# Weighing the next block's query terms inside the attention loop, and one pair sum moved between the halves of a reciprocal

## The chip, the core and the metric

The kernel runs on one core of a Trainium2 chip. Five engines matter here: TensorE (PE in the profile; its weight loads are PEld), VectorE (DVE), ScalarE (ACT), GpSimd (POOL) and SyncE (SP, which here only issues DMAs). Each engine works through its own instructions in order; semaphores tie them together. The metric is device time in microseconds of one launch. Before the change it is 10633.31 us, the median of three runs (10629.44 to 10641.02).

## The reference

The input is `x` of shape (4, 128, 64, 64). Layer 0 normalises it by groups and adds a convolution with a selective scan. Layer 1 reads the result as 4 images of 4096 tokens with 128 channels and adds two terms. The first of them, an additive attention, is what this change touches:

```python
def _L1_attn_ref(x, Wt, Wx, bh, Wa, ba):
    q = jnp.einsum('bld,ud->blu', x, Wt)
    k = jnp.einsum('bld,ud->blu', x, Wx)
    beta = jnp.tanh(q[:, :, None, :] + k[:, None, :, :] + bh)
    alpha = jnp.einsum('bsju,u->bsj', beta, Wa[:, 0]) + ba[0]
    alpha = jnp.tanh(alpha)
    alpha = jax.nn.softmax(alpha, axis=-1)
    c_r = jnp.einsum('bsj,bjd->bsd', alpha, x)
    return c_r
```

There are 32 hidden units u, and for every image 4096 x 4096 pairs (s, j), so the sum over u of `Wa[u] * tanh(q + k)` dominates. The second term is a recurrence over the tokens, in the function `_chunked`.

## The kernel before

Three functions follow one another: `_layer0`, `_rational` (the attention) and `_chunked` (the recurrence). The order of the instructions in each is written out by hand: what the Python code issues first comes first in its engine's queue.

**How the tanh is avoided.** The 32 hidden units are split into six groups, two of 6 units and four of 5. Within a group, the weighted sum of the tanh is a quotient of two sums of exponentials, one term for each choice of signs: 64 terms for 6 units, 32 for 5. Each term is a product of a factor of the query and a factor of the key. So for keys `F = exp(...)` and queries `E = exp(...)`, the denominator of a group is one matmul of F with E (tile `pd`), and the numerator is the same matmul with `cE`, which is E with each row multiplied by that term's weight `c_n` (tile `pn`). The function `weigh` makes `cE` from `E` with two VectorE instructions.

**The tiling.** A block is 512 queries (`QB`) of one image; there are 8 blocks for each of 4 images, 32 in all. Within a block the code goes through the 4096 keys in 32 tiles of 128 (`jt`). For each `jt` there are three units: "A" (the two groups of 6), "B1" and "B2" (two groups of 5 each). A unit's tile is 128 keys x 2 groups x 512 queries.

**The loop over the units.** For unit i, PE makes the denominators two units ahead and the numerators one unit behind. ACT inverts the denominator as exp(-ln d): line 1524 is the Ln, which also empties `pd`; line 1527 is the Exp, one unit later. DVE multiplies with the two numerators (`times`, line 1414, two instructions for a unit). POOL adds the units B1 and B2 to A (line 1533), which leaves two sums side by side, and DVE adds these to one another (`whole`, line 1518) and so finishes one row `A[:, jt, :]`. The tile of a unit A comes from the pool `ra` (4 buffers), that of a unit B from the pool `rb` (5 buffers).

`whole` for tile `jt - 1` is issued right after the second unit of tile `jt` has been multiplied, so that the loop itself finishes the tiles up to JT - 2 = 30.

**Work hung into the loop.** The dictionary `between` names small steps and the place (jt, position in jt) after which each is issued; `later` fills it. Here stand the matmuls, the maximum and the Exp of the next block's queries (`E_next`, from place (23, 2) and (25, 2) on), the layer norm of the next image, the last products of the block before with the values (`weighted`), and that block's closing division and its addition on POOL (line 1462).

**The end of a block.** After the loop, `weigh(E_next)` makes `cE` for the next block (line 1379). Then ACT takes the softmax's Tanh and Exp over the 32 finished rows in four parts (`PARTS`: rows 0 to 4, 12, 20 and 32; lines 1583 and 1584). Meanwhile `ahead` starts the next block: it makes the denominators of its first key tile and inverts them on DVE with `direct`, which takes a unit's two halves one after the other, each a reciprocal (line 1424) and a product with the numerator (line 1425). The sum `whole(31)` is issued once, after the first of these halves. Between the calls of `ahead`, PE does the products with the values of the parts that are already done (`weighted`, line 1557). `ahead(3)` ends with the denominators of the first two units of the next loop. In three of the 31 block ends the image changes, and then `all_keys` computes the next image's keys before `ahead`.

**Memory.** The pools of `_rational` are opened in a fixed order and lie in SBUF one after the other in that order; the pool `one` (1 buffer) holds `cE`, `two` (2 buffers) holds `xn` and `E`, `fp` holds F.

Of the kernel before, what the change touches and what calls it, by code (L numbers as in the profile page):

```python
# [8 lines left out]
F32 = mybir.dt.float32  # L9
# [6 lines left out]
P = 128  # L16
# [10 lines left out]
JT = L // P  # L27
# [36 lines left out]
QB = 512  # L64
# [1177 lines left out]
def _rational(ctx, tc, k, x1, xn1, x2, top, kept, ba):  # L1242
# [11 lines left out]
    one = ctx.enter_context(tc.tile_pool(name="none", bufs=1))  # L1254
    sb = ctx.enter_context(tc.tile_pool(name="nsb", bufs=2))
    ra = ctx.enter_context(tc.tile_pool(name="nra", bufs=4))
    rb = ctx.enter_context(tc.tile_pool(name="nrb", bufs=5))
    two = ctx.enter_context(tc.tile_pool(name="ntwo", bufs=2))
    fp = ctx.enter_context(tc.tile_pool(name="nf", bufs=1))
    kp = ctx.enter_context(tc.tile_pool(name="nk", bufs=1))  # L1260
    psD = ctx.enter_context(tc.tile_pool(name="npsD", bufs=2, space=PSUM))
    psN = ctx.enter_context(tc.tile_pool(name="npsN", bufs=3, space=PSUM))
# [111 lines left out]
        return exponent(pw, w_q, xn[:, s * QB : (s + 1) * QB], i, E[:, i, :])  # L1374

    def weigh(E):
        cE = one.tile([P, 2, QB], F32, name="cE")
        for i in range(2):
            nc.vector.tensor_scalar(cE[:, i, :], E[:, i, :], c_n[:, i : i + 1], None, ALU.mult)  # L1379
        return cE  # L1380
# [36 lines left out]
        pool, tag = (ra, "ra") if unit == "A" else (rb, "rb")  # L1417
        return pool.tile([P, 2, QB], F32, name=tag, tag=tag)

    def direct(d, ns, unit, then=None):  # L1420

        r = ratio(unit)
        for a in range(2):
            nc.vector.reciprocal(r[:, a, :], d[:, a, :])  # L1424
            nc.vector.scalar_tensor_tensor(r[:, a, :], r[:, a, :], 1.0 / LOWER, ns[a], ALU.mult, ALU.mult)
            if then is not None:
                then()
                then = None
        return r

    def order(jt):
# [50 lines left out]
    cE = weigh(E)  # L1482
# [8 lines left out]
    for b in range(B):  # L1491
        upcoming = None
        for s in range(nq):
# [11 lines left out]
            if more:  # L1505
                E_next = two.tile([P, 2, QB], F32, name="E")
                of = upcoming if turned else xn
                for i in range(2):
                    later(between, 23 + 2 * i, 2, zip(queries(E_next, of, (s + 1) % nq, i), (0, 1, 2)))
            ln_exp()  # L1510
            units = [(jt, pos, unit) for jt in range(start, JT) for pos, unit in enumerate(order(jt))]
            n = len(units)
            D = dict(enumerate(first))
# [6 lines left out]
            for i in range(n + 2):  # L1520
# [7 lines left out]
                if i >= 2:  # L1528
                    at, p, unit = units[i - 2]
                    r = R[at, p]  # L1530
                    times(r, N.pop(i - 2))
                    if p:
                        nc.gpsimd.tensor_tensor(R[at, 0], R[at, 0], R.pop((at, p)), ALU.add)  # L1533
                    if p == 1 and at > start:
                        whole(at - 1)
                forms = []
                if i + 2 < n:
# [12 lines left out]
            assert not between  # L1550

            if more:
                E, cE = E_next, weigh(E_next)
            ct = pw()

            def weighted(jt, ct=ct, xT=xT):
# [1 line left out]

            held = {}

            def ahead(step):
                if not more:
                    if step == 0:
                        whole(JT - 1)
                    return
                if step == 0:
                    held["A"], held["B1"] = lower("A", F, 0, E), lower("B1", F, 0, E)
                    held["A"] = direct(held["A"], upper("A", F, 0, cE), "A", lambda: whole(JT - 1))  # L1570
                elif step == 1:
                    held["B2"] = lower("B2", F, 0, E)
                    held["B1"] = direct(held["B1"], upper("B1", F, 0, cE), "B1")
                    nc.gpsimd.tensor_tensor(held["A"], held["A"], held["B1"], ALU.add)
                elif step == 2:
                    held["first"] = lower("A", F, 1, E)
                    r = direct(held["B2"], upper("B2", F, 0, cE), "B2")
                    nc.gpsimd.tensor_tensor(held["A"], held["A"], r, ALU.add)
                else:
                    held["first"] = held["first"], lower("B2", F, 1, E)  # L1580
# [283 lines left out]
```

## Time and profile before

| | |
|---|---|
| median of three runs | 10633.31 us |
| the profiled execution | 10622.87 us, span 10621.1 us |
| busy, of the span | PE 9213.9, DVE 9043.7, ACT 9094.5, POOL 8609.3 us |
| mean granted clock of TensorE | 0.942 of full speed |
| `_rational` | from about 3606 to about 10357 us of the span |
| one block, loop and end (block 7) | loop 177.67 us (5087.27 to 5264.94), end before it 30.42 us (5056.85 to 5087.27) |
| Ln, line 1524, into `rb` and `ra` | 1230 and 1219 ns each; ACT idle before them 26.9 and 52.6 us in all |
| `times`, line 1414 | 682 to 686 ns |
| `whole`, line 1518 | 759 ns, 993 times |
| POOL's sum, line 1533 | 2519 ns, 1986 times |
| `weigh`, line 1379 | 64 times, 479 to 2590 ns, median 1411 ns |

The profile is of one execution. Busy time is the time in which an engine worked; a duration of an instruction that follows closely on another can include some of its neighbour. "Idle before" is the time in which the engine stood still ahead of an instruction, and the arrow names what it waited for last. PE's clock is throttled by the hardware at times; the profile shows the share that was granted.

### The profile page before, as it was taken

How to read it: one execution, taken by the hardware profiler on the slowest of the kernel's cores; microseconds unless marked ns; L12 is line 12 of the kernel's file. 1: busy time of each engine (PE TensorE's matmuls, PEld its weight loads, DVE VectorE, ACT ScalarE, POOL GpSimd, SP SyncE). 2: the span in 40 equal slices, each digit the busy share in tenths (PEclk: the TensorE clock that was granted, in tenths of full speed). 3: DMA queues.
4: the chain of work that ended last, by engine and by line, in shares of the span. 5: the costliest groups of instructions: out<-in, count | busy, mean ns of one | idle time of the engine just before them, and what ended most of it. 6: DMA issues, size and time to landing. Idle time of an engine off the chain costs nothing.

```text
span 10621.1 us, 110120 instructions
## 1 busy us (share of the span) xinstructions
PE 9213.9 (87%) x35452; PEld 3226.5 (30%) x35452; DVE 9043.7 (85%) x10031; ACT 9094.5 (86%) x10279; POOL 8609.3 (81%) x3686
## 2 busy tenths in 40 slices
PE   7787787787777799999999999999999999999997
PEld 2121221222211233333333333333333333333334
DVE  7999999999999788888888888888888888888882
ACT  4566666766766799999999999999999999999995
POOL 7999899999999777788678778877888777767773
PEclk8898898898888999999999999999999999999998
DMA  6889889888888200000000000000000000000001
GB/s 150 200 191 213 189 193 212 194 197 209 198 199 203 71 4 4 4 4 7 4 4 4 7 4 4 7 4 4 4 7 4 4 3 5 3 3 3 5 2 66
DMA packets 228573, 739.50 MB, mean 70 GB/s; under 512 B 41536, under 2 KB 42368, under 8 KB 226448
## 3 DMA queue, kind: packets, MB, share of 16 engines
q1 hardware_dynamic: 224576, 730.76, 29.2%
q8 instruction: 280, 4.59, 0.2%
q14 instruction: 309, 2.53, 0.1%
q10 hardware_dynamic: 3408, 1.63, 0.1%
HBM read 609.15 MB, written 118.88 MB: 69 GB/s over the span
## 4 chain that ended last, share of the span: by engine, by line
PE 35%; ACT 21%; DVE 5%; issue 5%; POOL 1%; DMA 0%; DVEq 0%; POOLq 0%; ACTq 0%; SPq 0%
PE pd L1393 16%; PE pn L1393 10%; PE ct L1557 6%; ACT rb L1527 6%; ACT rb L1524 6%; ACT ra L1524 2%; ACT A L1583 2%; DVE rb L1414 2%; ACT ra L1527 2%; ACT A L1584 1%; DVE ra L1424 1%; PE vy L1758 1%; POOL ra L1533 0%; DVE cE L1379 0%; ACT E L1300 0%
## 5 line engine op out<-in xcount | busy, mean ns | idle before, releaser
L1533 POOL TENSOR_TENSOR ra<-ra,rb 128x1024 f32<-128x1024 f32 x1986 | 5000.9, 2519 | 813.0 <-ACT rb L1527 446.5
L1393 PE MATMUL pn<-cE,F 32*128 32x512 f32 (+1 forms) x12288 | 4602.5, 643 | 88.3 <-DVE rb L1414 78.0
L1393 PE MATMUL pd<-E,F 32*128 32x512 f32 (+1 forms) x12288 | 4037.8, 650 | 342.9 <-ACT ra L1524 239.8
L1414 DVE TENSOR_TENSOR rb<-rb,pn 128x512 f32<-128x512 f32 x3972 | 2543.4, 682 | 582.4 <-PE pn L1393 576.8
L1527 ACT ACTIVATE rb<-rb 128x1024 f32<-128x1024 f32 x1986 | 2513.6, 1270 | 0.0
L1524 ACT ACTIVATE rb<-pd 128x1024 f32<-128x1024 f32 x1986 | 2443.0, 1230 | 26.9 <-PE pd L1393 24.6
L786 POOL TENSOR_TENSOR dBu<-dtdu,bbcc 128x1024 f32<-128x1024 f32 x1024 | 2391.4, 2365 | 88.8 <-DMA dtdu<-dd 58.2
L1393 PEld LDWEIGHTS pd<-E,F 32*128 32x128 f32 (+1 forms) x12288 | 1209.9, 186 | 2257.2 <-ACT ra L1524 972.1
L1393 PEld LDWEIGHTS pn<-cE,F 32*128 32x128 f32 (+1 forms) x12288 | 1420.9, 186 | 1317.3 <-DVE rb L1414 647.0
L1414 DVE TENSOR_TENSOR ra<-ra,pn 128x512 f32<-128x512 f32 x1986 | 1356.1, 686 | 384.8 <-PE pn L1393 287.4
L826 PE MATMUL py<-h,gather 128*32 128x512 f32 x4096 | 1190.6, 677 | 391.7 <-POOL h L812 372.9
L1527 ACT ACTIVATE ra<-ra 128x1024 f32<-128x1024 f32 x993 | 1258.0, 1267 | 0.0
L1524 ACT ACTIVATE ra<-pd 128x1024 f32<-128x1024 f32 x993 | 1210.4, 1219 | 52.6 <-PE pd L1393 43.7
L781 ACT ACTIVATE pa<-dtdu,a_neg 128x1024 f32<-128x1024 f32 x1024 | 1143.6, 1117 | 34.7 <-DMA dtdu<-dd 11.2
L802 DVE TENSOR_TENSOR_SCAN pa<-pa,carry,dBu 128x1024 f32<-128x1024 f32 x480 | 1125.4, 2345 | 32.3 <-ACT pa L781 22.9
L1557 PE MATMUL ct<-A,xT 128*128 128x512 f32 x2048 | 1046.4, 639 | 10.5 <-ACT A L1584 10.5
L812 POOL TENSOR_TENSOR h<-h,bbcc 128x1024 f32<-128x1024 f32 x381 | 899.3, 2360 | 121.8 <-ACT carry L810 104.9
L810 ACT COPY carry<-pa 128x1 f32<-128x1 f32 x643 | 103.0, 160 | 883.9 <-DVE h L809 883.3
L809 DVE TENSOR_TENSOR h<-pa,bbcc 128x1024 f32<-128x1024 f32 x643 | 787.7, 1225 | 61.7 <-PE py L826 1.7
L1518 DVE TENSOR_TENSOR A<-ra 128x512 f32<-128x512 f32 x993 | 753.9, 759 | 35.9 <-POOL ra L1533 31.6
L802 DVE TENSOR_TENSOR_SCAN h<-pa,carry,dBu 128x1024 f32<-128x1024 f32 x288 | 673.2, 2341 | 21.3 <-PE py L826 10.6
L826 PEld LDWEIGHTS py<-h,gather 128*32 128x32 f32 x4096 | 221.8, 116 | 1255.9 <-issue 529.0
(306 smaller groups left out, 8282.2 us busy)
## 6 DMA issues: line engine op xcount, KB each, us to landing
bbcc<-bcd SPq DMA_DIRECT2D x1024, 256.0 KB, 7.7
dtdu<-ddd SPq DMA_DIRECT2D x1008, 256.0 KB, 7.8
ddd<-dd SPq DMA_DIRECT2D x63, 1024.0 KB, 5.1
src<-src SPq DMA_DIRECT2D x60, 512.0 KB, 9.7
xs<-in_x_dram SPq DMA_DIRECT2D x32, 256.0 KB, 7.3
src<-xs SPq DMA_DIRECT2D x16, 512.0 KB, 6.2
bcd<-bc SPq DMA_DIRECT2D x64, 128.0 KB, 1.9
src<-xsT SPq DMA_DIRECT2D x16, 512.0 KB, 5.4
```

What stands on the lines that cost most here:

```text
L781: nc.scalar.activation(dA, its[m].DT[r][:, 0, :], AF.Exp, scale=a)
L786: nc.gpsimd.tensor_tensor(dBu, its[m].DT[r][:, 1, :], its[m].BC[q][:, 0, :], ALU.mult)
L802: nc.vector.tensor_tensor_scan(to[:, step], dA[:, step], live.pop(("dBu", u))[:, step], 0.0 if m % nch == 0 else its[m - 1].carry[:, col : ...
L809: nc.vector.tensor_tensor(h, dA, cc, ALU.mult)
L812: nc.gpsimd.tensor_tensor(h, h, cc, ALU.mult)
L826: nc.tensor.matmul(it.y[to, c], gather, live["h", v][:, c], start=False, stop=(q == QS - 1))
L1393: nc.tensor.matmul(ps[a], F[lo:hi, i, jt * P : (jt + 1) * P], side[lo:hi, i, :], start=True, stop=True)
L1414: nc.vector.tensor_tensor(r[:, a, :], r[:, a, :], ns[a], ALU.mult)
L1524: nc.scalar.activation(r, D.pop(i), AF.Ln, scale=LOWER)
L1527: nc.scalar.activation(r, r, AF.Exp, scale=-1.0)
L1533: nc.gpsimd.tensor_tensor(R[at, 0], R[at, 0], R.pop((at, p)), ALU.add)
L1557: nc.tensor.matmul(ct, xT[:, jt, :], A[:, jt, :], start=(jt == 0), stop=(jt == JT - 1))
```

## The change

- `weigh(E_next)` is no longer issued between the loop and the end of a block but inside the loop, at place (26, 2), one unit after the place of the last Exp of `E_next`. The result is kept until the loop is over. As the old `cE` is still read by then, `cE` moves to the pool `two` and has two buffers.
- The sum `whole(30)` is no longer issued in the loop. `direct` now takes one step for each of its two halves: after the first half comes `whole(30)`, after the second `whole(31)`. In the very last block, which has no `direct`, both are issued together.
- The pool `rb` has 4 buffers in place of 5, and `fp` is opened ahead of `two`, so the tiles lie at other addresses.

```diff
-    rb = ctx.enter_context(tc.tile_pool(name="nrb", bufs=5))
+    rb = ctx.enter_context(tc.tile_pool(name="nrb", bufs=4))
+    fp = ctx.enter_context(tc.tile_pool(name="nf", bufs=1))
     two = ctx.enter_context(tc.tile_pool(name="ntwo", bufs=2))
-    fp = ctx.enter_context(tc.tile_pool(name="nf", bufs=1))
...
     def weigh(E):
-        cE = one.tile([P, 2, QB], F32, name="cE")
+        cE = two.tile([P, 2, QB], F32, name="cE")
...
-    def direct(d, ns, unit, then=None):
+    def direct(d, ns, unit, then=(None, None)):
 
         r = ratio(unit)
         for a in range(2):
             nc.vector.reciprocal(r[:, a, :], d[:, a, :])
             nc.vector.scalar_tensor_tensor(r[:, a, :], r[:, a, :], 1.0 / LOWER, ns[a], ALU.mult, ALU.mult)
-            if then is not None:
-                then()
-                then = None
+            if then[a] is not None:
+                then[a]()
         return r
...
+                later(between, 26, 2, [(lambda E_next=E_next: held.update(cE=weigh(E_next)), 0)])
             ln_exp()
+            held = {}
...
-                    if p == 1 and at > start:
+                    if p == 1 and start < at < JT - 1:
                         whole(at - 1)
...
-                E, cE = E_next, weigh(E_next)
+                E, cE = E_next, held["cE"]
...
                 if not more:
                     if step == 0:
+                        whole(JT - 2)
                         whole(JT - 1)
                     return
                 if step == 0:
                     held["A"], held["B1"] = lower("A", F, 0, E), lower("B1", F, 0, E)
-                    held["A"] = direct(held["A"], upper("A", F, 0, cE), "A", lambda: whole(JT - 1))
+                    held["A"] = direct(held["A"], upper("A", F, 0, cE), "A", (lambda: whole(JT - 2), lambda: whole(JT - 1)))
```

## The prediction

> **What bounds the kernel now.** I read the page's costliest groups first, then the timelines of a good block (it ends at 5056.85) and a poor one (ends at 9294.58), then the granted clock by stretches. The first fence is from the page, the rest from a query of one line and from timelines and windows.
>
> ```profile
> L1524 ACT ACTIVATE rb<-pd 128x1024 f32<-128x1024 f32 x1986 | 2443.0, 1230 | 26.9 <-PE pd L1393 24.6
> L1524 ACT ACTIVATE ra<-pd 128x1024 f32<-128x1024 f32 x993 | 1210.4, 1219 | 52.6 <-PE pd L1393 43.7
> ...
> 5087.27:5264.94 177.67, 166.87 (x778) 60.95 (x777) 145.22 (x225) 177.00 (x192) 153.91 (x62) 1.00 0.02 5
> 5056.85:5087.27 30.42, 28.88 (x68) 10.34 (x68) 29.71 (x18) 30.26 (x10) 8.15 (x4) 0.83 0.00 0
> 9324.99:9506.21 181.22, 170.22 (x780) 63.33 (x779) 144.38 (x224) 175.64 (x189) 153.91 (x62) 0.98 0.01 4
> ```
>
> In a window's row the fourth bracketed engine is ACT and the figure after POOL is PE's clock. In the good block ACT works 177.00 of the loop's 177.67 us and 30.26 of the 30.42 us at the block's end: ACT sets the time, and only its waits can be won. In the loops they are 26.9 + 52.6 = 79.5 us in all, 0.75% of the span. The poor loop waits 5.58 us.
>
> Read over the 32 loops, ACT's waits fall into three places: 26.6 us in a loop's first 6 us; a floor of 0.67 us a loop at key tile 23, plus 23 us more there in some blocks; 9 us in the last loop.
>
> ```profile
> L1379 DVE TENSOR_SCALAR cE<-E,consts x64: 479/1411/2590, 3611.6 to 10144.7; 128x512 f32<-128x512 f32 x64
> ...
> 5059.15 3.90 DVE L1379 TENSOR_SCALAR cE<-E,consts 128x512 f32<-128x512 f32 x2
> 5062.97 3.35 DVE L1424 RECIPROCAL ra<-pd 128x512 f32<-128x512 f32 x1
> 5087.32 0.69 DVE L1425 SCALAR_TENSOR_TENSOR rb<-rb,pn 128x512 f32<-128x512 f32 x1
> ...
> 5081.28 7.13 PE L1557 MATMUL ct<-A,xT 128*128 128x512 f32 x16
> 5088.35 1.13 PE L1393 MATMUL pd<-E,F 32*128 32x512 f32 x4
> 5089.64 1.13 PE L1393 MATMUL pd<-E,F 32*128 32x512 f32 x4 [0.16 <-ACT ra L1524]
> ...
> 9308.78 1.22 PE L1393 MATMUL pd<-E,F 32*128 32x512 f32 x2 [5.21 <-DVE ra L1424]
> 9329.62 1.02 ACT L1524 ACTIVATE rb<-pd 128x1024 f32<-128x1024 f32 x1 [2.31 <-PE pd L1393]
> ...
> 5208.05 2.82 DVE L1518 TENSOR_TENSOR A<-ra 128x512 f32<-128x512 f32 x1 [0.89 <-POOL ra L1533]
> 5211.52 0.69 PE L1393 MATMUL pn<-cE,F 64*128 64x512 f32 x1 [2.14 <-DVE rb L1414]
> 9453.20 1.02 ACT L1524 ACTIVATE ra<-pd 128x1024 f32<-128x1024 f32 x1 [2.67 <-PE pd L1393]
> ...
> 9306.70:9313.50 6.80, 4.72 (x11) 1.69 (x12) 6.59 (x5) 6.77 (x3) 0.00 (x0) 0.50 0.00 0
> 9450.10:9456.90 6.80, 5.85 (x19) 2.16 (x20) 4.38 (x8) 4.06 (x5) 2.52 (x2) 0.50 0.00 0
> ```
>
> See here that the two instructions of `weigh` hold DVE for 3.90 us at the block's end, that in the good block PE still arrives just in time (0.16 us idle), and that in the poor one PE stands 5.21 us for DVE's reciprocal, runs at half clock for 6.8 us afterwards, and makes ACT wait 2.31 us. The second half-clock stretch follows a stall of PE behind DVE at key tile 23.
>
> **The clock decides the rest.** Over all loops and block ends: PE gaps of 1.53 to 1.57 us at a block's end were followed by no fall of the clock that they began; of the 2.15 us gaps at tile 23, 12 of 32 were; of the 12 gaps of 2.9 us or more, all. A fall lasts 3.4 us or a multiple. At tile 23 a 3.4 us fall cost ACT 0.48 us (the wait at 5445.34), a 6.8 us one 2.67 + 0.49 + 0.07 - 0.67 = 2.56 us.
>
> The Trainium skill, TensorE: Matmul & The Clock Gate, Part 1 (the HAM clock gate), states that a free-running window of about 3.4 us is watched and that PE's clock halves after an idle one; its section on HAM oscillation wants no PE gap above about 3.4 us. The rows agree on the length but are stricter: gaps of 2.15 us are enough when the work around them is sparse. By the page's limit no gap that I work out below would cost anything, and the sum would be some 38 us lower; I go by the rows.
>
> **Part 1, `weigh` leaves the block's end.** DVE loses 3.90 us there. Its reciprocal can't start at 5059.15, as its `pd` comes from matmuls that begin at 5058.26 and run at half clock, about 1.06 us a half: 5059.3, so 3.65 us earlier than 5062.97. `whole(30)` comes back as 0.6 us after the first half, so all after it is 3.05 us earlier: the last product ends at 5084.96 instead of 5088.01. ACT gains nothing of that in the block's end, because its Tanh and Exp run without a gap. But PE is no longer held by DVE's reciprocals, only by ACT's Exp of each part. In the poor block, whose first matmuls run at full clock, its chain is then: Exp of the second part ends 9307.07, 16 products with the values in 7.13 us to 9314.2 (Exp of the third part: 9314.32), 2.1 us of `pd` and `pn`, 16 products in 7.13 us, 1.1 us of `pd`: done at 9324.6. The next matmul needs ACT's first Ln, done at 9327.2: a new gap of 2.6 us, just where the loop starts. In the good block the first matmuls run at half clock and the first 8 products end at 5069.49; 1.1 + 7.13 + 2.1 + 7.13 + 1.1 us later is 5088.0, against 5089.6: a gap of 1.6 us.
>
> What goes: PE's late arrival, which is the 26.6 us less what the change can't touch: 0.4 in the first loop, 2.3 in the three loops after a change of image. That gives -23.9. ACT's second Ln no longer waits 0.1 us for PE: 28 x 0.1 = -3.
> What is late next: PE's clock in the loop's first microseconds. The Ln that needs the first new denominator comes 1.97 us after the Ln that frees its buffer (5089.48 to 5091.45); in the steady loop it is 2.8 us (5045.36 to 5048.16). With 0.8 us less in reserve a fall costs more than the middle, 1.5, between the 0.48 and 2.56 us at tile 23: I take 1.7. A gap of 1.6 to 2.6 us, with 1.1 us of sparse matmuls on either side, lies nearest to the 2.15 us row (12 of 32) and touches the 2.9 us row (all). The sparse neighbours pull it to the latter: I take 8 in 10. 28 x 0.8 x 1.7 = +38; ends 0 and 28 x 2.56 = +72.
>
> **Part 2, `weigh` in the loop.** On DVE it stands behind the multiplication of unit (26, 0), with the rest of tile 26 and `whole(25)` queued behind it; PE waits for those to get its `pn` back, and POOL for its next sum. Alone an instruction took 479 ns; beside POOL's sums 1398 and 2579 ns. In the block at 5234 DVE reaches this place at about 5235.5, POOL's running sum ends at 5237.04, and its next sum needs a multiplication behind `weigh`. So I take 1.5 us of waiting and 2 x 0.48: done at 5238.0 where the multiplication started at 5236.50, DVE 1.5 us late; ends 0.96 and 2 x 2.59 us. At tile 23 DVE is 0.89 + 2.13 = 3.0 us late and ACT loses 0.67. Half of that lateness, with PE idle 0.72 us in that tile anyway, gives 0 to 0.67; I take 0.25 x 31 = +8, ends 0 and +21.
> The Trainium skill, SBUF — State Buffer, Who interferes with whom, says the port pair that VectorE shares with GpSimd is held for a whole instruction. The 2579 ns beside sums of 2519 ns agree; by that rule alone both instructions could wait out a sum, 5.2 us, which is the far end just named.
>
> **Part 3, the sum of tile 30.** One instruction of 0.6 us moves past the last multiplication and one reciprocal; row 30 is wanted by the Tanh at 5076.49, over 10 us after it. It is in the 3.05 us above. After a change of image DVE's chain is PE's gate and has no `weigh` in it (its reductions wait for ACT), so there it adds 0.6 us: 3 x 0.6 = +2.
>
> **Part 4, memory.** With 4 buffers an Ln into `rb` needs POOL's sum of four B units before. That sum ends 2.0 us ahead in the steady loop (5040.60 against 5042.61) and 0.5 us at the narrowest, at 9448.05: no wait, 0; if POOL lags 2 us more in a loop, its excess is ACT's. The shifted `xn` is loaded on SP's queue at 3572.52 and first used by a matmul at about 3606: over 30 us of cover, 0; beyond that it would cost one for one.
>
> **Phase.** Good blocks repeat each 208.1 us, close to 61 of the 3.41 us steps in which the clock changes, and so keep missing a fall at tile 23. Other block times break this. By where a step's edge lay in the 32 gaps at tile 23, about a third of the phases have no fall, nearly half a short one, a fifth a long one: (0 + 0.47 x 0.48 + 0.2 x 2.56) = 0.7 us above the floor. The 23 loops with a next image have 0.2 now (+0.5 each); the 7 without have 2.4, and, being sparser, I give them 1.5 (-0.9 each): 11.5 - 6.3 = +5; ends -22 (none falls) and +31 x 1.9 = +59.
>
> **Sum.** -23.9 - 3 + 38 + 8 + 2 + 0 + 5 = +26 us. On the profiled 10622.9 that is 10649; the median shown is 10.4 us above this execution, so 10659 us.
>
> **Rivals.**
> 1. No change to speak of: falls at the loop start are as rare or as short as at tile 23. 28 x 0.5 = 14 instead of 38: +2 us, 10635. For it: 1.53 us gaps never cost anything. Against: the sparse matmuls.
> 2. Faster: the new gap never lowers the clock. It decides below a gap of some 1.6 us, for which the last products would have to end a microsecond later than worked out. -23.9 - 3 + 8 + 2, and the phase between -22 and +5: -12 to -39, its middle 10607. For it: ACT really loses 2.3 us in each of the last seven loops. Against: PE's chain is bound by ACT's Exp, and 26 us is all there is.
> 3. Slower still: `weigh` makes PE stall at tile 26 as at 23, with a fall in most blocks: 31 x 1.5 = 47 instead of 8: 10698. For it: 2.59 us for one instruction. Against: POOL has nothing to start behind it.
> That the moves do nothing at all, DVE being hidden, would end beside rival 1.
>
> **How the numbers follow.** Forecast 0.40, rival 1 0.25, rival 2 0.25, rival 3 0.10. About 0.2% (21 us) is what a measurement of this kernel can tell from no change. The forecast lies at +26 us, so a part of it, 0.05, falls below that bound: slower 0.35 + 0.10 = 0.45, same 0.25 + 0.05 = 0.30, faster 0.25. The range reaches from rival 2's better end, 10594, to rival 3, 10698; the forecast's own is 10640 to 10685.
>
> **What would show it.** No `weigh` between the loop and the first reciprocal, which starts 3 to 4 us earlier relative to ACT's table load. PE idle 1.5 to 2.7 us before the loop's third denominator, and half clock there. No 5 us gaps for the reciprocal of A. `weigh` at tile 26 taking some 2.4 us for its pair. ACT's waits ahead of the Ln near 100 us instead of 79.5. I am wrong if the clock stays full at the loop start, if blocks settle on one period that misses both falls, or if `rb` shows waits for POOL.

## The result, and the profile after

The changed kernel takes 10792.27 us (median of four runs, 10790.77 to 10809.64) against 10633.52 us (10629.44 to 10641.02): the ratio is 1.0157, 95% interval 1.0145 to 1.0168. That is slower by 159 us, and outside the range I gave. The profiled execution took 10809.64 us, the longest of the four; its span is 10807.9 us, 186.8 us more than that of the one profiled before. PE's mean granted clock fell from 0.942 to 0.930.

The first fence holds four of the page's costliest groups after the change; behind the second bar stands the idle time just before them and what ended most of it.

```profile
L1525 ACT ACTIVATE rb<-pd 128x1024 f32<-128x1024 f32 x1986 | 2398.4, 1208 | 45.8 <-PE pd L1393 40.5
L1525 ACT ACTIVATE ra<-pd 128x1024 f32<-128x1024 f32 x993 | 1190.1, 1198 | 189.2 <-PE pd L1393 146.9
L1519 DVE TENSOR_TENSOR A<-ra 128x512 f32<-128x512 f32 x993 | 881.6, 888 | 50.9 <-POOL ra L1534 50.0
L1534 POOL TENSOR_TENSOR ra<-ra,rb 128x1024 f32<-128x1024 f32 x1986 | 4962.6, 2501 | 1076.5 <-DVE rb L1414 672.6
```

ACT waits 45.8 + 189.2 = 235.0 us ahead of its Ln, 155.5 us more than the 79.5 us before, out of the 186.8 us between the two profiled executions. Most of it is in the Ln of the A units (189.2 against 52.6 us). Two other rows moved with it: one pair sum (`whole`) takes 888 ns on average where it took 759, and POOL stands idle 1076.5 us where it stood 813.0, most of that for DVE's multiplications.

Next the windows of one block, its loop and its end, and the row of `weigh` (shortest, median and longest duration in ns).

```profile
4268.29:4452.12 183.83, 169.54 (x769) 58.91 (x770) 149.89 (x224) 177.69 (x193) 150.81 (x62) 0.97 0.02 5
4452.12:4482.54 30.42, 30.42 (x73) 10.76 (x70) 27.59 (x18) 30.26 (x10) 8.78 (x4) 0.83 0.00 0
```

```profile
L1379 DVE TENSOR_SCALAR cE<-E,consts x64: 472/482/1944, 3613.0 to 10288.9; 128x512 f32<-128x512 f32 x64
```

The block's end still takes 30.42 us with ACT busy for 30.26 of them: nothing is won or lost there. DVE's work in it went from 29.71 to 27.59 us. The loop went from 177.67 to 183.83 us, while ACT's work in it stayed at 177.69 us: it waits 6.14 us. Over all 32 loops the time grew by 181 us. `weigh` costs one instruction of 1.8 to 1.9 us and one of 0.48 us, much as forecast.

So where in the loop does ACT wait? I added up all its idle times by place, over the 32 loops (us; with the waits ahead of the Exp of the next queries, 8 us after the change). A tile of the loop takes 5.58 us, and here and below the tiles of a wait or a pair sum are counted by time: the last column begins some 136 us into a loop, and `weigh` stands at about 150.

| kernel | first 10 us | up to tile 21 | tiles 22 to 24 | behind them |
|---|---|---|---|---|
| before | 26.6 | 0 | 44.6 | 8.0 |
| after | 47.3 | 5.1 | 49.9 | 140.5 |

Most of the loss lies behind tile 24, where `weigh` now stands: 111.8 of the 140.5 us come behind `weigh` itself, 3.6 us for each of the 31 loops that have one. Another 17.3 us come between tile 24 and `weigh`, in loops where the stall at tile 23, described below, starts a chain or a long fall of PE's clock, and 11.3 us in the last loop, which has no `weigh`. The timeline of the block above shows it, from `weigh` on (start and duration in us; in brackets the idle time and what ended it):

```profile
4413.32 0.68 DVE L1519 TENSOR_TENSOR A<-ra 128x512 f32<-128x512 f32 x1
4413.55 5.12 POOL L1534 TENSOR_TENSOR ra<-ra,rb 128x1024 f32<-128x1024 f32 x2 [0.50 <-ACT rb L1528]
...
4417.12 2.22 DVE L1379 TENSOR_SCALAR cE<-E,consts 128x512 f32<-128x512 f32 x2
4419.26 1.27 DVE L1414 TENSOR_TENSOR rb<-rb,pn 128x512 f32<-128x512 f32 x2
...
4420.46 0.68 DVE L1519 TENSOR_TENSOR A<-ra 128x512 f32<-128x512 f32 x1
4420.68 7.46 POOL L1534 TENSOR_TENSOR ra<-ra,rb 128x1024 f32<-128x1024 f32 x3 [2.01 <-DVE rb L1414]
...
4425.86 2.84 DVE L1519 TENSOR_TENSOR A<-ra 128x512 f32<-128x512 f32 x1 [0.33 <-POOL ra L1534]
4428.62 1.27 DVE L1414 TENSOR_TENSOR rb<-rb,pn 128x512 f32<-128x512 f32 x2
4429.35 0.88 PE L1393 MATMUL pn<-cE,F 64*128 64x512 f32 x1 [2.08 <-DVE rb L1414]
4430.06 2.35 POOL L1534 TENSOR_TENSOR ra<-ra,rb 128x1024 f32<-128x1024 f32 x1 [1.92 <-DVE rb L1414]
4431.16 1.02 ACT L1525 ACTIVATE ra<-pd 128x1024 f32<-128x1024 f32 x1 [2.27 <-PE pd L1393]
```

The clock of PE before and behind its stand, in two windows (us; the figure after POOL is PE's clock):

```profile
4426.20:4429.60 3.40, 1.32 (x6) 0.49 (x8) 3.40 (x3) 2.69 (x3) 1.94 (x1) 1.00 0.01 2
4429.70:4433.10 3.40, 3.40 (x15) 1.02 (x14) 1.47 (x3) 1.94 (x2) 2.35 (x1) 0.50 0.00 0
```

Read the timeline downwards. In the undisturbed tile (the first two rows) the pair sum starts 0.23 us ahead of POOL's next sum and takes 0.68 us, and POOL does two sums and then pauses for half a microsecond. `weigh` holds DVE for 2.22 us. POOL has nothing to add until the multiplication behind `weigh` is done, and stands 2.01 us. Then it is late and does three sums without a pause. The pair sum of the next tile needs the second of the three. It waits for that, and by then POOL is in its third: the pair sum takes 2.84 us in place of 0.68. The multiplications queued behind it are 2.1 us late; PE, which wants its `pn` back, stands 2.08 us, and then works at half its clock for 3.4 us; and ACT, which has no denominator left, waits 2.27 us. POOL has again been idle 1.92 us, so it starts late again, and 14 us further on the same happens once more (a pair sum of 2.82 us at 4439.85, an Ln that waits 2.64 us at 4445.44).

Of all pair sums, 34 took more than 1.5 us before, 31 of them at tile 22 or 23; after the change 95 do, 64 of them elsewhere, and in 24 of the 31 loops the second pair sum behind `weigh` is one of these. The stand of PE and the fall of its clock can be told apart in these 24. In 8 of them the clock falls only when the Ln is about to start, or not at all, and the Ln waits 1.62 to 1.64 us; in the other 16 it falls earlier, and the Ln waits 1.90 to 2.67 us. So the stand makes the greater part of the wait, and the clock adds 0.3 to 1.0 us.

### The profile page after: what moved, and what is told of

Its sections match the earlier page's. It is cut to its first block, busy times and chain, and to the rows that moved or that the text cites. A ratio compares the mean times of both kernels' runs of the same rounds, so it can differ in the third digit from the quotient of the medians.

```text
span 10807.9 us, 109384 instructions
## 1 busy us (share of the span) xinstructions
PE 9367.0 (87%) x35452; PEld 3219.1 (30%) x35452; DVE 9118.9 (84%) x10031; ACT 9112.3 (84%) x10279; POOL 8572.1 (79%) x3686
## 4 chain that ended last, share of the span: by engine, by line
PE 39%; ACT 20%; issue 4%; DVE 3%; POOL 0%; DMA 0%; DVEq 0%; SPq 0%; POOLq 0%; ACTq 0%
PE pd L1393 18%; PE pn L1393 13%; PE ct L1558 6%; ACT rb L1528 5%; ACT rb L1525 5%; ACT ra L1525 3%; ACT A L1583 2%; ACT A L1584 2%; ACT ra L1528 2%; DVE rb L1414 1%; PE vy L1758 1%; PE vy L1769 0%; DVE A L1519 0%; ACT E L1300 0%; PE pd L1346 0%
## 5 line engine op out<-in xcount | busy, mean ns | idle before, releaser
L1534 POOL TENSOR_TENSOR ra<-ra,rb 128x1024 f32<-128x1024 f32 x1986 | 4962.6, 2501 | 1076.5 <-DVE rb L1414 672.6
L1393 PE MATMUL pn<-cE,F 32*128 32x512 f32 (+1 forms) x12288 | 4808.8, 661 | 214.8 <-DVE rb L1414 213.2
L1393 PE MATMUL pd<-E,F 32*128 32x512 f32 (+1 forms) x12288 | 4212.6, 665 | 244.8 <-ACT ra L1525 188.2
L1528 ACT ACTIVATE rb<-rb 128x1024 f32<-128x1024 f32 x1986 | 2467.2, 1244 | 0.0
L1525 ACT ACTIVATE rb<-pd 128x1024 f32<-128x1024 f32 x1986 | 2398.4, 1208 | 45.8 <-PE pd L1393 40.5
L1393 PEld LDWEIGHTS pn<-cE,F 32*128 32x128 f32 (+1 forms) x12288 | 1474.4, 191 | 1609.8 <-DVE rb L1414 938.2
L1393 PEld LDWEIGHTS pd<-E,F 32*128 32x128 f32 (+1 forms) x12288 | 1255.3, 191 | 2160.1 <-ACT ra L1525 909.9
L1525 ACT ACTIVATE ra<-pd 128x1024 f32<-128x1024 f32 x993 | 1190.1, 1198 | 189.2 <-PE pd L1393 146.9
L1528 ACT ACTIVATE ra<-ra 128x1024 f32<-128x1024 f32 x993 | 1234.7, 1243 | 0.0
L1519 DVE TENSOR_TENSOR A<-ra 128x512 f32<-128x512 f32 x993 | 881.6, 888 | 50.9 <-POOL ra L1534 50.0
```

The lines of the kernel that those rows point to most:

```text
L1393: nc.tensor.matmul(ps[a], F[lo:hi, i, jt * P : (jt + 1) * P], side[lo:hi, i, :], start=True, stop=True)
L1519: nc.vector.tensor_tensor(A[:, jt, :], r[:, 0, :], r[:, 1, :], ALU.add)
L1525: nc.scalar.activation(r, D.pop(i), AF.Ln, scale=LOWER)
L1528: nc.scalar.activation(r, r, AF.Exp, scale=-1.0)
```

## The experiments

The theory (A in the expectations): POOL is made late by `weigh`, and the pair sum then meets POOL's next sum. Each expectation says what its rivals are: that the layout or the moved sum is at fault, that the kind of instruction matters, or that any hold on DVE costs in proportion. All times are medians of timed runs; ratios are to the kernel before, timed beside them on the same chip.

### Which part of the change costs it

The first run keeps everything but the place of `weigh`; the second keeps the place and the layout, and leaves the sum of tile 30 in the loop; the third is the kernel before with the new layout alone; the fourth is the kernel before with two multiplications like those of `weigh` put into an early tile.

```diff
# e1: the changed kernel with weigh back at the block's end
-                later(between, 26, 2, [(lambda E_next=E_next: held.update(cE=weigh(E_next)), 0)])
...
-                E, cE = E_next, held["cE"]
+                E, cE = E_next, weigh(E_next)
# e2: the changed kernel with the sum of tile 30 back in the loop
-                    if p == 1 and start < at < JT - 1:
+                    if p == 1 and at > start:
...
-                        whole(JT - 2)
...
-                    held["A"] = direct(held["A"], upper("A", F, 0, cE), "A", (lambda: whole(JT - 2), lambda: whole(JT - 1)))
+                    held["A"] = direct(held["A"], upper("A", F, 0, cE), "A", (lambda: whole(JT - 1), None))
# e3: the kernel before with rb at 4 buffers, fp opened ahead of two, cE in two
# e4: the kernel before with
+                for i in range(2):
+                    later(between, 10, 2, [(lambda i=i, E=E, E_next=E_next: nc.vector.tensor_scalar(E_next[:, i, :], E[:, i, :], c_n[:, i : i + 1], None, ALU.mult), 0)])
```

> All of the change, except that the query terms are weighed at the end of the block again. Theory A (the two instructions in the loop make POOL late, so that the sums of tiles 26 and 28 or 29 meet POOL's sum, and PE and ACT stall behind them): both late stalls of a loop are gone, the kernel is within 30 us of before, 10620 to 10665 us. Theory B (the loss comes from the new idle time of PE at the loop start and from the moved sum of tile 30): half or more of the 159 us stays, 10700 us or more. Theory C (four buffers of rb or the new layout make ACT wait): nearly all of it stays, 10760 to 10800 us.

> The weighing in the loop and the new layout, but the sum of tile 30 is in the loop as before and the reciprocal has one step as before. Theory A: 10760 to 10810 us, as the changed kernel; the sum of tile 30 in the loop can meet POOL's sum as well and may add some 2 us a loop. Theory B: 10700 us or less.

> Only the memory: four buffers of rb, the new order of the pools, two buffers of cE; every instruction at its old place. Theories A and B: as before, 10625 to 10645 us. Theory C: 10760 us or more.

> The kernel before, to which two more VectorE instructions of the same size and form are added in every loop with a next block, at tile 10, into a buffer that is overwritten later; the result is unchanged. Nothing else is moved. Theory A: at tiles 10 to 13 the same chain as after the change, the pair takes some 2.3 us, one or two sums of a tile take 2.8 us instead of 0.7, ACT waits 2 to 5 us a loop: 10700 to 10790 us. If only DVE's own time counts, its slack of about 1 us a tile takes it up: within 20 us of before.

| run | us (lowest to highest) | ratio, 95% | pair sums over 1.5 us | ACT's waits behind tile 24 |
|---|---|---|---|---|
| e1, `weigh` at the end | 10635.2 (10622.4 to 10644.4) | 1.0002 [0.9992, 1.0012] | 33 | 8.3 |
| e2, `weigh` in the loop, sum of tile 30 too | 10800.4 (10794.6 to 10805.9) | 1.0160 [1.0143, 1.0177] | 101 | 132.2 |
| e3, layout alone | 10631.5 (10625.4 to 10636.4) | 1.0001 [0.9992, 1.0011] | 34 | 8.7 |
| e4, twin of `weigh` at tile 10 | 10773.4 (10771.9 to 10796.0) | 1.0141 [1.0124, 1.0158] | 83 | 38.2 |

The layout and the moved sum cost nothing that can be measured. Putting `weigh` into the loop costs all of it. And the place need not be tile 26: with two such multiplications at tile 10 the second pair sum behind them is long in 29 loops, and there are 104.6 us of waits between there and tile 21, where the kernel before has none.

### What kind of hold, and how long

Is it the multiplication, which reads and writes SBUF beside POOL's sums, or only that DVE is late? The kernel before got four maximum reductions at tile 10 in place of the multiplications. Then the length: one and two of the same reductions, in a kernel freed of the stall at tile 23 (v1, below).

```diff
# e5: the kernel before; d1 and d2: v1, with range(1) and range(2)
+                for i in range(4):
+                    later(between, 10, 2, [(lambda E=E, E_next=E_next: nc.vector.tensor_reduce(E_next[:, 0, 0:1], E[:, 0, :], AX.X, ALU.max), 0)])
```

> The kernel before, with four maximum reductions of one 512-column row block each put on VectorE at key tile 10 of every block that has a next one; their output is overwritten later and the result is unchanged. They read one operand and write one column; I expect some 0.6 us each, 2.4 us in all, as long as the pair of multiplications in the loop (2.2 us).
> Theory A (VectorE is late by some 2 us, so GpSimd's next sum is released late, runs back to back with the following ones, and the pair sum that needs it meets the next sum; the kind of instruction that made VectorE late does not matter): as with the two multiplications at tile 10, some 30 pair sums over 1.5 us at tile 12 and ACT waits of 180 to 210 us ahead of the Ln; 10750 to 10800 us.
> Theory C (it is the multiplications themselves, which read and write SBUF beside GpSimd's sums, that start the chain): about the time before, 10620 to 10650 us, with no long pair sums at tile 12.

> The kernel before with GpSimd's late addition at the loop's end (10582.6 us when last timed), and one maximum reduction (0.71 us on VectorE, as measured with four of them) at key tile 10 of every block that has a next one; its output is overwritten later.
> Theory A (a pair sum is lengthened when GpSimd is still behind at the second pair sum after the delay; GpSimd's spare time is some 0.6 us a tile): GpSimd is 0.7 us late and has caught up by then: no long pair sums, 10575 to 10600 us.
> Theory B (VectorE's lateness as such costs, in proportion): a quarter of what four reductions cost beyond the time before (203 us), some 50 us: 10620 to 10645 us.

> As the run with one reduction, with two of them: 1.42 us on VectorE.
> Theory A: GpSimd is 1.4 us late, 0.6 us are won back by the second pair sum behind it, 0.8 us stay: that pair sum meets GpSimd's next sum in most loops (about 30 over 1.5 us), ACT waits at least 1.6 us for it, as behind weigh in the changed kernel: 10630 to 10720 us.
> Theory B: half of 203 us: 10670 to 10700 us, without long pair sums.
> If the limit lies above 1.4 us: 10575 to 10600 us.

| DVE held for | run | us | its base | second pair sum behind it long | waits up to tile 21 |
|---|---|---|---|---|---|
| 0.68 us | d1 | 10586.0 (10583.3 to 10589.2) | v1, 10582.6 | 0 of 31 loops | 0 |
| 1.40 us | d2 | 10682.1 (10671.1 to 10709.3) | v1, 10582.6 | 29 | 92.5 |
| 2.2 us | e4 | 10773.4 | before, 10629.5 | 29 | 104.6 |
| 2.84 us | e5 | 10834.0 (10819.9 to 10850.6) | before, 10631.1 | 7 (in 19 others the fourth) | 130.0 |

The ratios are 0.9957 [0.9940, 0.9973] for d1, 1.0045 [1.0028, 1.0061] for d2 and 1.0188 [1.0171, 1.0205] for e5. Rows of d1's timeline and of d2's show the threshold. In each fence the first row holds the reductions, the first POOL row shows the pause behind them, and the last pair sum shown is the second behind them:

```profile
4311.89 0.68 DVE L1516 TENSOR_REDUCE E<-E 128x1 f32<-128x512 f32 x1
4313.90 5.13 POOL L1540 TENSOR_TENSOR ra<-ra,rb 128x1024 f32<-128x1024 f32 x2 [0.45 <-ACT rb L1534]
...
4319.24 0.68 DVE L1525 TENSOR_TENSOR A<-ra 128x512 f32<-128x512 f32 x1
4319.47 5.13 POOL L1540 TENSOR_TENSOR ra<-ra,rb 128x1024 f32<-128x1024 f32 x2 [0.43 <-ACT rb L1534]
```

```profile
4320.98 1.40 DVE L1516 TENSOR_REDUCE E<-E 128x1 f32<-128x512 f32 x2
4323.72 7.44 POOL L1540 TENSOR_TENSOR ra<-ra,rb 128x1024 f32<-128x1024 f32 x3 [1.18 <-DVE rb L1414]
...
4328.88 2.83 DVE L1525 TENSOR_TENSOR A<-ra 128x512 f32<-128x512 f32 x1 [0.31 <-POOL ra L1540]
...
4333.88 1.02 ACT L1531 ACTIVATE ra<-pd 128x1024 f32<-128x1024 f32 x1 [1.62 <-PE pd L1393]
```

The chain needs no multiplication: reductions start it too. It is not in proportion either. Theory B gave 10620 to 10645 us for one reduction, but its ratio to the kernel before is that of its base, 0.9957 against 0.9955. Behind one reduction POOL is not late at all: it pauses 0.45 us as in every tile, and what ends the pause is ACT. DVE has pauses of its own in a tile (0.39, 0.49 and 0.24 us), which can take the hold up. Behind holds of 1.40, 2.23 and 2.84 us POOL pauses 1.17, 2.02 and 2.62 us (medians over the loops), so it is late by the hold less about 0.67 us. That lateness grows evenly; the cost doesn't. With 0.73 us of it the chain starts in 30 of 31 loops and costs some 96 us (1.0045 against 0.9955). At 2.84 us the loss begins in another way, and e5 missed theory A for that: it is above the range, with 7 long second pair sums where some 30 were expected. PE stands 0.94 us at once, ahead of any long pair sum, and in most loops its clock then falls: in the block read in detail an Ln waits 2.56 us at 4335.11 while the pair sum behind the reductions takes 0.69 us.

Could `weigh` be made short enough? Its halves were put at two places, and its columns were taken in another order:

```diff
# e7: the two multiplications apart
-                later(between, 26, 2, [(lambda E_next=E_next: held.update(cE=weigh(E_next)), 0)])
+                cE_next = two.tile([P, 2, QB], F32, name="cE")
+                for i in range(2):
+                    later(between, 26 + 3 * i, 2, [(lambda i=i, E=E_next, cE=cE_next: nc.vector.tensor_scalar(cE[:, i, :], E[:, i, :], c_n[:, i : i + 1], None, ALU.mult), 0)])
...
-                E, cE = E_next, held["cE"]
+                E, cE = E_next, cE_next
# e8: in weigh
-            nc.vector.tensor_scalar(cE[:, i, :], E[:, i, :], c_n[:, i : i + 1], None, ALU.mult)
+            to, of = (x[:, i, :].rearrange("p (a b) -> p b a", a=2) for x in (cE, E))
+            nc.vector.tensor_scalar(to, of, c_n[:, i : i + 1], None, ALU.mult)
```

> The changed kernel with the two multiplications of weigh apart: the first at key tile 26, the second at tile 29.
> Theory A with each of them waiting for GpSimd's running sum (1.83 us for the first of the pair in the changed kernel): each makes GpSimd late by about 1.8 us and starts a chain of its own: 10760 to 10830 us, long pair sums in most loops behind both.
> If the second only took 0.48 us, or a delay below some 2 us is harmless: 10630 to 10700 us.

> The changed kernel with weigh's operands read and written in another order of the columns (first half and second half in turn), which gives the same values; the elements are then no longer next to each other in the order in which VectorE takes them.
> If that takes the multiplication out of the mode that waits for GpSimd's sum: some 0.6 to 0.7 us for each, 1.3 to 1.4 us for the pair instead of 2.2 us, without a wait. Theory A: GpSimd is still 1.4 us late and the second pair sum behind it meets the next sum; 10700 to 10790 us. If 1.4 us is below the limit: the chain is gone and the time goes back to 10620 to 10680 us.
> If it waits just as before: 10780 to 10810 us.

Neither helps. Apart, as theory A had it, the first multiplication takes 1.83 us and the second 2.41 us, beside POOL's sums, where one alone takes 0.48 us: 10788.9 us (10787.2 to 10792.9), 1.0148 [1.0131, 1.0165]. The second pair sum behind the first multiplication is long in 27 loops, and 22 more long ones follow the second multiplication. In the other order one alone takes 0.74 us, and in the loop the first still waits (2.1 and 0.74 us): 10824.9 us (10824.1 to 10835.0), 1.0182 [1.0165, 1.0199], above all three of the cases that I had written down. Whether that order changes how VectorE takes its operands, the run doesn't tell.

### Does the pair sum cause the wait, or only go with it?

`weigh` stays at tile 26, and the pair sums behind it (rows 26 to 29) are left out. In the loop nothing else changes; DVE has 0.68 us a tile less to do for it.

```diff
-                    if p == 1 and start < at < JT - 1:
+                    if p == 1 and start < at < (JT - 1 if b + s == 0 else 27):
```

> The changed kernel, in which the pair sums of tiles 26 to 29 are left out of every block but the first (those rows keep what the last block left there, so this part of the attention is not computed). weigh stays at key tile 26; VectorE, GpSimd and PE do all else as before. VectorE has 4 times 0.68 us a block less to do, but it does not set the time.
> Theory A (the second pair sum behind weigh, held 2.8 us by GpSimd's next sum, is what makes PE stand and ACT wait): ACT's waits behind tile 25 fall from 140 us to under 30 us; 10610 to 10670 us.
> Theory B (VectorE's delay of 2.2 us, or the three sums in a row on GpSimd, suffice without the pair sum): the waits stay above 80 us; 10720 to 10790 us.

10676.1 us (10663.7 to 10686.3), ratio 1.0044 [1.0029, 1.0058]: 116 us less than the changed kernel (1.0157), a little above the range of theory A and far below that of B. ACT's waits behind tile 24 fall from 140.5 to 41.2 us, those behind `weigh` itself from 111.8 to 21.8 us. Six rows of one block's timeline:

```profile
4399.42 2.23 DVE L1379 TENSOR_SCALAR cE<-E,consts 128x512 f32<-128x512 f32 x2
4401.01 0.70 PE L1393 MATMUL pd<-E,F 32*128 32x512 f32 x2 [0.72 <-ACT ra L1525]
4402.30 1.74 PE L1393 MATMUL pn<-cE,F 32*128 32x512 f32 x3 [0.16 <-DVE rb L1414]
4402.77 0.68 DVE L1519 TENSOR_TENSOR A<-ra 128x512 f32<-128x512 f32 x1
4402.99 9.90 POOL L1534 TENSOR_TENSOR ra<-ra,rb 128x1024 f32<-128x1024 f32 x4 [2.02 <-DVE rb L1414]
4412.16 0.70 PE L1393 MATMUL pd<-E,F 32*128 32x512 f32 x2 [0.67 <-ACT ra L1525]
```

`weigh` holds DVE as before, POOL is late as before (2.02 us) and now does four sums in a row, but PE waits for ACT again, not for DVE. So the pair sum that meets POOL is the cause of about 100 of the 140 us. That DVE has less to do can hardly be the reason: in the changed kernel PE's stand of 2.08 us is about what the long pair sum took beyond its 0.68 us. Of the other 33 us (41.2 against the 8.0 of the kernel before) some 17 are the hold itself: in 12 of the 31 loops PE's clock falls about 4 us behind the start of `weigh`, and an Ln waits 1.3 to 1.6 us at 7.5 us behind it. Most of the rest belongs to chains that start at tile 23 in the last loops. The windows of one of the 12 loops, where `weigh` starts at 5245.00:

```profile
5245.50:5249.20 3.70, 2.82 (x14) 0.87 (x12) 3.70 (x6) 3.70 (x6) 1.68 (x2) 0.97 0.00 0
5249.20:5252.60 3.40, 3.40 (x12) 0.97 (x12) 1.71 (x3) 2.00 (x3) 3.32 (x2) 0.53 0.02 5
```

PE was at work for 2.82 of the 3.70 us ahead of the fall, with no pause above 0.8 us, and got half the clock (0.53) for the next 3.4 us all the same. In 13 other loops of this run the same stretch, with the same longest pause of 0.72 us and the same 2.8 us of work, was followed by no fall; what decides between the two is not shown.

### The stall at tile 23, and a place for `weigh`

The kernel before has the same meeting at tile 23, behind POOL's extra addition (line 1462, 1.27 us). v1 is that kernel with the addition and its store issued at the loop's end. e6 has `weigh` at a place with no pair sum behind it in the loop, v2 has both, and v3 puts `weigh` on POOL at that place and the addition into the middle of the block's end.

```diff
# e6: the changed kernel
-                later(between, 26, 2, [(lambda E_next=E_next: held.update(cE=weigh(E_next)), 0)])
+                later(between, 31, 2, [(lambda E_next=E_next: held.update(cE=weigh(E_next)), 0)])
# v1: the kernel before; v2: e6 with the same
+        def add():
             nc.gpsimd.tensor_tensor(xr, xr, held["rec"], ALU.add)
             nc.sync.dma_start(x2[b, :, blocks[s]], xr)
...
+        owed.append(add)
...
             assert not between
+            while owed:
+                owed.pop(0)()
...
# v3: weigh with nc.gpsimd in place of nc.vector at (31, 2); owed is emptied behind ahead(1)
```

> The changed kernel, with the two multiplications of weigh five tiles later, at key tile 31 in place of 26, behind the multiplication of the last tile's first unit.
> Theory A (the loss comes from the pair sums that follow a late GpSimd in the loop): behind this place the loop has no pair sum left, so long pair sums go back to some 34, ACT's waits ahead of the Ln to 75 to 100 us, and the time to 10610 to 10650 us.
> Theory B (whatever holds VectorE for 2 us inside the loop costs ACT some 5 us a block, through PE and its clock, wherever it is): 10760 to 10800 us.
> Theory D (the new layout or the sums between the halves of the inversion cost it together with the loop's place): 10760 to 10800 us as well.

> The kernel before, with GpSimd's addition into xr and its store moved from key tile 21 of the loop to the loop's end, where GpSimd is idle.
> Theory A (GpSimd being 1.26 us late at tile 21 makes the pair sum at tile 22 to 23 meet the next sum, and PE's 2.15 us gap and the falls of the clock come from that): the 31 long pair sums there are gone, ACT's waits at tile 23 (0.67 us a loop and 23 us more in some loops, 44 us in all) go with them: 10585 to 10615 us.
> Rival (the wait at tile 23 comes from the closing steps on VectorE, the inversion in four parts and the product, or from the projections of the next queries at the same tile): unchanged, 10625 to 10640 us.

> The changed kernel with weigh at key tile 31 and GpSimd's addition into xr with its store at the loop's end.
> Theory A: both effects add: no long pair sums at tile 23 and none behind weigh; ACT's waits ahead of the Ln 35 to 60 us, 10570 to 10615 us. If the gap in PE ahead of the loop's first units makes the clock fall there (some 1 us a block), the upper end.
> Theory B: 10730 to 10780 us.

> The changed kernel with weigh on GpSimd, at key tile 31 (ahead of its last two sums of the loop), and GpSimd's addition into xr with its store in the middle of the block's end, where GpSimd waits 15 us.
> Theory A: no long pair sums in the loop, as in the run with weigh on VectorE at tile 31 and the addition at the loop's end (10577 us); VectorE is 2.3 us earlier at the block's end, and if that is what makes PE late at the start of the loops (30 us of ACT's waits there), a part of it goes: 10545 to 10575 us.
> Rival (GpSimd's multiplications, some 1 to 1.3 us each, make the last sum late enough for the block's end to wait, or the earlier VectorE opens gaps in PE ahead of the loop and the clock falls there): 10580 to 10640 us.

| run | us (lowest to highest) | ratio, 95% | long pair sums | waits: first 10 us | tiles 22 to 24 | behind |
|---|---|---|---|---|---|---|
| e6 | 10674.5 (10670.8 to 10682.7) | 1.0043 [1.0027, 1.0060] | 42 | 32.2 | 55.6 | 33.6 |
| v1 | 10582.6 (10579.9 to 10587.1) | 0.9955 [0.9938, 0.9972] | 4 | 38.5 | 2.9 | 2.4 |
| v2 | 10577.1 (10573.3 to 10581.6) | 0.9950 [0.9933, 0.9966] | 2 | 30.2 | 1.2 | 2.7 |
| v3 | 10560.7 (10558.0 to 10563.6) | 0.9937 [0.9920, 0.9953] | 15 | 14.2 | 1.9 | 2.7 |

Of v3's 15 long pair sums 13 stand in the block ends, outside the loops.

v1 settles the stall at tile 23: with POOL on time there, its 31 long pair sums are gone and 42 us of waits with them. The undisturbed tile, in v1's timeline, where the kernel before shows 2.82 us for the pair sum at 5208.05:

```profile
5205.43 0.69 DVE L1523 TENSOR_TENSOR A<-ra 128x512 f32<-128x512 f32 x1
5205.60 5.20 POOL L1538 TENSOR_TENSOR ra<-ra,rb 128x1024 f32<-128x1024 f32 x2 [0.21 <-ACT rb L1532]
```

e6 missed theory A's range: the long pair sums behind `weigh` went, as expected, but the block's period changed with it, and the meeting at tile 23 now fell on a drop of the clock in most loops and started chains of its own in the last ones. With that meeting removed (v2), `weigh` at tile 31 is harmless. v3 beats both kernels, by 0.63% against the kernel before. Its rows in the page, of the Ln and of `weigh`:

```profile
L1530 ACT ACTIVATE rb<-pd 128x1024 f32<-128x1024 f32 x1986 | 2641.7, 1330 | 4.1 <-PE pd L1393 4.0
L1530 ACT ACTIVATE ra<-pd 128x1024 f32<-128x1024 f32 x993 | 1311.1, 1320 | 17.1 <-PE pn L1393 13.6
```

```profile
L1379 POOL TENSOR_SCALAR cE<-E,consts x62: 1552/1562/1578, 3807.9 to 10092.3; 128x512 f32<-128x512 f32 x62
```

ACT waits 21.2 us ahead of its Ln in place of 79.5. A multiplication takes 1.56 us on POOL, three times what it takes on DVE alone, and no wait of ACT in the loop shows its cost. The gain over v2 is 16 us by the medians, which come from two chips, and the intervals of the two ratios overlap. It can be the earlier DVE or the later addition, which the run does not separate; the waits of the first 10 us, which fell by 16.0 us, speak for the first.

## Why the prediction was wrong, point by point

**Part 2, `weigh` in the loop: this step failed.** Its duration was right (about 2.4 us forecast, 2.22 us measured), and so was DVE's lateness (1.5 us; POOL's pause of 2.01 instead of 0.50 us says the same). The step ended there. It put the price at 0.25 us a block, 8 us in all, with 21 us as its far end; 111.8 us of waits were measured behind `weigh`, 3.6 us for each of 31 blocks, where the same stretch of the kernel before has 2.4 us in all. What it left out is the second round: it named "POOL for its next sum" as one who waits, and didn't ask what a late POOL does to the pair sum a tile later. It halved the 0.67 us of tile 23 in proportion to DVE's lateness, while the cost has a threshold, at a hold between 0.68 and 1.40 us. And the row that shows the mechanism was in its own fence: the pair sum of 2.82 us at 5208.05, behind a POOL delayed by 1.27 us. I read that as DVE's lateness at tile 23, and did not see POOL's addition as its origin.

**Rival 3** had the right direction and half the chain ("`weigh` makes PE stall at tile 26 as at 23, with a fall"), at 1.5 us a block where 3.6 were measured. What I held against it, "POOL has nothing to start behind it", was the mistake: POOL starts nothing at once, and three sums in a row afterwards.

**Part 1, the block's end: the mechanism is shown, best in other kernels.** In the kernel before, the first reciprocal starts 6.1 to 6.9 us behind ACT's table load, and it was to start 3 to 4 us earlier. In 16 of the 28 ordinary block ends (those without a change of image) it starts at 3.0 to 5.0 us. In nine it starts later than before, because a loop that ends in a chain lets PE and DVE into the block's end late; two rows, from the timeline of such a block, whose first reciprocal starts 8.2 us behind the table load:

```profile
4886.55 3.36 DVE L1424 RECIPROCAL ra<-pd 128x512 f32<-128x512 f32 x1 [1.33 <-PE pd L1393]
...
4914.35 1.02 ACT L1525 ACTIVATE rb<-pd 128x1024 f32<-128x1024 f32 x1 [3.29 <-PE pd L1393]
```

The nine loops behind these ends start with such a wait of about 3.3 us, 30 us together; that the sum of the loop starts (47.3 us) is near the 41 that follow from the prediction's terms is chance. Where the chains are gone, both terms can be read. PE's late arrival does go: v3's loop starts wait 14.2 us, of which 10.1 are falls of the clock and nearly all the rest the three changes of image; x1's wait 25.7 us, 20.8 of them behind falls and nearly all the rest at the changes of image. That is the -23.9. And PE does get a new gap ahead of the loop's third denominator, 0.5 to 1.6 us in v3 and 0.9 to 2.9 us in x1 (1.6 or 2.6 forecast); in v3 falls follow 10 of 13 gaps from 1.2 us on. The changed kernel has such a gap, above 1.1 us, in 8 of its 28 ordinary loop starts, with a fall behind 6 of them; one of these:

```profile
6007.20 1.13 PE L1393 MATMUL pd<-E,F 32*128 32x512 f32 x4
6009.50 1.53 PE L1393 MATMUL pd<-E,F 32*128 32x512 f32 x4 [1.18 <-ACT ra L1525]
...
6014.27 1.02 ACT L1525 ACTIVATE ra<-pd 128x1024 f32<-128x1024 f32 x1 [1.11 <-PE pn L1393]
```

The price was 38 us. In the changed kernel the six falls cost some 6 us in the loops' first 10 us. With pair sums left out (x1) 23 of 28 loop starts have a fall, and 32 us of waits come from them, 1.4 each: the 20.8 us, and 11.3 us further on in the same loops. In v3 it is 11 of 28 and 10 us. So the size nearly holds for one block period and is about four times too large for another.

**Part 3, the sum of tile 30,** was given +2 us: the three block ends with a change of image went from 145.7 to 146.6 us together, and with the sum back in the loop the time is the same (1.0160 against 1.0157). **Part 4, memory,** was given 0, and the layout alone gives 1.0001 [0.9992, 1.0011].

**Phase** was given +5 us at tile 23; the waits there went from 44.6 to 49.9 us. The agreement says little. The period of the blocks changed far more than I had reckoned with, and chains and long falls of the clock that began at tile 23 now ran on past tile 24: those 17.3 us ahead of `weigh`, where the kernel before has none, and 11.3 us in the last loop in place of 5.6. The prediction counts 32 gaps at tile 23, but 31 loops have one: the first loop has no block before it to close.

**Rivals 1 and 2** both lacked the loop's chain as well. What rival 2 hoped for, that freeing the block's end pays, shows only where the chains are out of the way: v3, which also moves POOL's addition, comes to 0.9937. With `weigh` left at the block's end the rest of the change is worth 1.0002.

The Trainium skill, SBUF — State Buffer, Who interferes with whom, says that a VectorE instruction with two SBUF inputs contends with a GpSimd one that reads SBUF, and that whoever is first keeps the port for its whole instruction. The pair sum's 2.82 us, 0.68 us and most of a 2.5 us sum of POOL, agrees; I cited that section for `weigh` alone, which was the wrong instruction to ask it about.

## What to carry to other kernels

When an instruction is put into a loop that two engines share tightly, follow the delay through one more turn: who is late behind the one that waits, and which later instruction will then meet it. Such a loop can have a threshold, not a slope: here a hold of 0.68 us was free, and one of 1.40 us cost more than twice its own length, in a chain that can repeat. If the profile before holds one long instruction where all its like are short, find out what delayed its partner before costing a new delay; here the same delay was worth 48 us as a gain.

## What the runs showed of the hardware that I had not expected

PE's granted clock fell without any pause above 0.8 us, where PE was at work for 2.82 of 3.70 us, in 12 of x1's 31 loops, while 13 others with the same work had no fall; I had looked only at pauses of 1.5 us and more. At v3's loop starts falls followed gaps from 1.2 us on, once one of 0.85 us, while three gaps of 1.57 to 1.59 us in the same run had none; in the changed kernel a gap of 2.59 us there and one of 1.62 us had none either.

A single-source multiplication on DVE whose columns were taken out of order took 0.74 us in place of 0.48 and still waited for POOL's sum (2.1 us for the first of a pair), while reductions of the same operand, 0.70 us each, never waited.
